# Graph attention on one core: scores and weights in one SBUF tile, one exponential in place, and a second PSUM bank for the transposes

## The chip, the core and the metric

The kernel runs on one core of a Trainium2 chip. The time is the device time of one execution in microseconds (us). A kernel is timed in several runs, and the median counts. One further execution is taken by the hardware profiler; the profile and the trace are of that one.

The core has five engines that run their own instruction streams and wait for each other by semaphores: PE (TensorE, matmul; PEld is its loading of the stationary operand), DVE (VectorE), ACT (ScalarE), POOL (GpSimd) and SP (SyncE, which here only issues transfers). Two on-chip memories matter here: SBUF, where most tiles live, and PSUM, where PE writes its products; the kernel divides PSUM by banks.

## The reference, cut to what matters

`x` has 16 batches of 1024 rows of 512, `adj` is one 1024 x 1024 matrix of zeros and ones that all batches share. There are 8 heads of 64.

```python
h = jnp.maximum(_layernorm(x, axis=-1), 0.0)
q = (h @ Wq + bq).reshape(b, n, H, HD)          # k and v alike
scores = jnp.einsum('bihd,bjhd->bhij', q, k) / jnp.sqrt(jnp.float32(HD))
scores = scores + mask[None, None, :, :]        # mask: -1e9 where adj == 0
weights = jax.nn.softmax(scores, axis=-1)
out = x + jnp.einsum('bhij,bjhd->bihd', weights, v).reshape(b, n, H * HD)
```

## The kernel before

A row of `adj` has few ones, so the kernel doesn't form the full matrix of scores. At the start it sorts the rows by their number of neighbours and makes a list of neighbours for each row. The sorted rows form 8 tiles of 128; tile 0 has the rows with most neighbours, up to 11 slots per row there and 2 in tile 7 (`CAPS`, line 41). What doesn't fit in tile 0's slots is cut into pieces of 4 neighbours, up to 128 pieces, which form a tile of their own (number -1 in `UNITS`, line 47).

**Per batch** the kernel does this. Each tile of `x` is loaded (`load_x`, line 558), normalised (`stats`, `variance`, `power`, `shift` and `norm`, lines 568 to 599; `norm` is on ACT), transposed by PE into a PSUM bank (`flip`, line 601: four transposes) and copied to SBUF by ACT (`unflip`, line 608). From the transposed tile PE makes keys and values (`proj_kv`, line 618), ACT copies them to SBUF (`evict_kv`), and SP stores them to a table in device memory (`store_kv`, line 629). There are three such tables, used in turn.

Then come 14 **units** (`UNITS`), each 2 to 4 neighbour slots of one tile. For a unit:

- `queries` (line 779): PE makes the tile's queries, in PSUM.
- `gather` (line 790): POOL gathers one row of keys and values per slot by an indirect transfer; the row's own slot comes by a plain transfer from SP. A unit's rows go into one of 6 buffers `g`.
- `multiply` (line 804) and `score` (line 809): DVE multiplies keys by the query and sums each head's 64 products. The sums go into the tile `scores`, **one PSUM bank for all slots of all units**.
- `exponent` (line 814): ACT takes the exponential. For tiles 7 to 4 (`SHARES`, in all batches but the last) it does so in place, in PSUM. For the others it writes the exponential to the SBUF tile `weights`, and then takes it **a second time**, in place in PSUM, for those slots that DVE will weigh.
- For tiles 7 to 4, `row_sums` (line 882) and `share` (line 825) on DVE turn exponentials into shares at once, from PSUM into `weights`.
- `weigh_s` (line 837): ACT multiplies a slot's values by its weight, 8 instructions of 64 columns. `weigh_v` (line 830): DVE does this for one slot of most units, reading the factors from `weights` (tiles 7 to 4) or from `scores` in PSUM (the others).
- `fold` (line 843) and `join` (line 848) add slots on DVE and POOL; tile 0, its pieces, and in the last batch all tiles, are added by PE in a PSUM bank instead (`add_up`, line 854, pool `acc` of two banks).
- `row_sums`, `scale` (line 892), `residual` on POOL and `put_out` finish a tile.

The pieces need a path of their own: `more` (line 874) on DVE sums the pieces' exponentials, and `pass_on` (line 879), a matmul of 8 columns on PE, brings these sums to the rows that own the pieces. It writes them into one extra column group of the `scores` bank, from where `row_sums` of tile 0 reads them.

**The order.** All engines' streams are written out in advance. `plan_of` (line 168) lists each operation with its engine, an assumed length, a **place** and what it needs; a unit of place is one of the 14 units, so a batch is 14. `Plan.ordered` (line 93) then plays it through: whenever an engine is free, it takes the ready operation of lowest place whose buffers are free (`POOLS`, line 72, says how many each pool has). The result is a fixed sequence per engine. At run time an instruction that must wait holds all that stand behind it on its engine. The plan knows of buffers but not that `scores` is one bank; semaphores are put in afterwards, by which data and which banks two instructions share.

The PSUM pools have eight banks: transposes 1 (`pht`), keys and values 2, queries 2, accumulators 2, `scores` 1.

## Time and profile before

| | |
|---|---|
| median of 3 runs | 1873.38 us (1863.66 to 1876.34) |
| the profiled execution | 1871.36 us |
| its span, first to last instruction | 1869.7 us |
| mean granted PE clock | 0.951 of full speed |
| instructions | 19763 |
| moved by DMA | 539.98 MB, 289 GB/s in the mean |

How to read the lines of the profile: a group of instructions has its line in the kernel, engine, operation, the tiles it writes `<-` reads, the shapes and `xcount`; then the busy time and the mean length of one in ns; then how long its engine sat idle just before these instructions, and what ended that (`<-ACT scores L823` means: an instruction of line 823 on ACT that writes `scores`). A timeline row has start, length, engine, line, operation, tiles, and in brackets the idle time before it. A row of a table by stretches has the stretch, its length, the busy time and number of instructions of PE, PEld, DVE, ACT and POOL, the granted clock, the share of the DMA engines, and GB/s. In a list of waits each row has who waited for whom, the total in us, how often, and the longest. A line that begins with `x624: 933/947/2034` gives least, median and greatest length in ns.

### The profile page before, as it was taken

The page shows a single profiled execution, that of the slowest core. Times are in us where ns is not written, and L with a number is a line of the kernel's source. Part 1 is how long each engine was busy: PE and PEld are TensorE (multiplying, and loading weights), DVE is VectorE, ACT ScalarE, POOL GpSimd, SP SyncE. Part 2 cuts the span into 40 slices and gives each one's busy share as a digit, 9 for nine tenths or more (in the row PEclk, how much of TensorE's full clock was granted, in tenths as well). Part 3 has the DMA queues.
Part 4 walks back from the last instruction along what each step waited for, and adds up shares of the span by engine and source line. Part 5 has one row for each costly group of instructions (what it writes and reads, how often), then busy time and mean ns, then how long its engine had stood idle before and what let it go on. Part 6 is the DMA issues. An engine that isn't in the chain of part 4 may idle for free. (4 is left out here: it accounts for less than half of the span.)

```text
span 1869.7 us, 19763 instructions
## 1 busy us (share of the span) xinstructions
PE 1653.7 (88%) x4301; PEld 762.9 (41%) x4301; DVE 1542.8 (83%) x1887; ACT 1508.6 (81%) x5661; POOL 1290.3 (69%) x1230
## 2 busy tenths in 40 slices
PE   5968699897989889897999979998898979989795
PEld 2434344443444444343444434444443434434331
DVE  5767779878898888988888788888888888889886
ACT  4337788889898888988887899988788888889864
POOL 4545668776787767776786867777676767767573
PEclk9989899998999999998999989999998999999898
DMA  5365789887898888888898878989787888988793
GB/s 214 119 254 200 289 301 315 317 295 281 307 333 313 314 301 298 299 293 295 304 336 308 294 275 306 327 313 326 271 314 270 300 304 310 329 285 315 264 329 134
DMA packets 151783, 539.98 MB, mean 289 GB/s; under 512 B 18908, under 2 KB 18908, under 8 KB 151656
## 3 DMA queue, kind: packets, MB, share of 16 engines
q0 software_dynamic: 111888, 399.09, 60.5%
q1 hardware_dynamic: 39768, 139.56, 20.6%
q8 instruction: 36, 0.59, 0.1%
q14 instruction: 91, 0.75, 0.1%
HBM read 437.85 MB, written 100.72 MB: 288 GB/s over the span
## 5 line engine op out<-in xcount | busy, mean ns | idle before, releaser
L841 ACT ACTIVATE g<-g,weights 128x64 f32<-128x64 f32 x4768 | 1185.4, 339 | 27.5 <-issue 15.8
L797 POOL DMA_INDIRECT g<-kv,index x624 | 628.7, 1007 | 248.7 <-issue 180.2
L616 PE MATMUL pq<-wq,hT 128*128 128x512 f32 x1024 | 471.0, 603 | 0.0
L807 DVE TENSOR_TENSOR g<-g,pq 128x2048 f32<-128x2048 f32 (+2 forms) x208 | 396.9, 1912 | 72.8 <-PE pq L616 42.9
L812 DVE TENSOR_REDUCE scores<-g 128x32 f32<-128x2048 f32 (+2 forms) x224 | 433.8, 1937 | 26.8 <-ACT scores L823 18.9
L616 PE MATMUL pk<-wk,hT 128*128 128x512 f32 x960 | 443.8, 606 | 0.0
L616 PE MATMUL pv<-wv,hT 128*128 128x512 f32 x960 | 431.6, 592 | 0.0
L846 DVE TENSOR_TENSOR g<-g 128x512 f32<-128x512 f32 (+1 forms) x285 | 267.0, 938 | 52.9 <-ACT g L841 39.1
L616 PEld LDWEIGHTS pq<-wq,hT 128*128 128x128 f32 x1024 | 200.2, 196 | 226.2 <-issue 221.2
L616 PEld LDWEIGHTS pk<-wk,hT 128*128 128x128 f32 x960 | 188.6, 196 | 211.7 <-issue 207.1
L616 PEld LDWEIGHTS pv<-wv,hT 128*128 128x128 f32 x960 | 182.4, 190 | 215.7 <-issue 212.4
L846 POOL TENSOR_TENSOR g<-g 128x512 f32<-128x512 f32 x105 | 137.4, 1308 | 111.2 <-DVE g L846 106.3
L908 POOL DMA_INDIRECT out_dram<-x,perm x128 | 137.6, 1075 | 79.1 <-DMA out_dram<-x,perm 28.4
L606 PE MATMUL pht<-ident,h 128*128 128x128 f32 x512 | 92.2, 310 | 86.5 <-ACT h L599 54.4
L564 POOL DMA_INDIRECT x<-in_x_dram,perm x128 | 136.6, 1067 | 36.1 <-issue 31.1
L606 PEld LDWEIGHTS pht<-ident,h 128*128 128x128 f32 x512 | 69.9, 159 | 168.0 <-ACT h L599 73.8
L864 PE MATMUL acc<-g,ident 128*128 128x512 f32 x176 | 101.3, 687 | 21.7 <-POOL g L846 12.1
L599 ACT ACTIVATE h<-x,shift,rstd 128x512 f32<-128x512 f32 x120 | 93.3, 809 | 32.4 <-DVE shift L589 31.3
L611 ACT COPY hT<-pht 128x512 f32<-128x512 f32 x128 | 74.1, 579 | 51.4 <-PE pht L606 27.4
L905 POOL TENSOR_TENSOR x<-x,o 128x512 f32<-128x512 f32 x68 | 90.0, 1324 | 21.9 <-DVE o L896 21.1
L627 ACT COPY kvt<-pk 128x512 f32<-128x512 f32 x120 | 68.9, 574 | 41.7 <-PE pk L616 33.6
L835 DVE TENSOR_TENSOR g<-g,scores 128x512 f32<-128x512 f32 (+1 forms) x104 | 73.8, 710 | 30.6 <-ACT scores L823 28.0
(226 smaller groups left out, 1196.6 us busy)
## 6 DMA issues: line engine op xcount, KB each, us to landing
g<-kv SPq DMA_DIRECT2D x128, 512.0 KB
kv<-kvt SPq DMA_DIRECT2D x120, 512.0 KB
g<-kv,index POOLq DMA_INDIRECT x624
adj<-in_adj_dram SPq DMA_DIRECT2D x8, 512.0 KB
x_first<-in_x_dram SPq DMA_DIRECT2D x8, 256.0 KB
x<-in_x_dram,perm POOLq DMA_INDIRECT x128
out_dram<-x,perm POOLq DMA_INDIRECT x128
wk<-in_L_gnn_Wk_dram SPq DMA_DIRECT2D x1, 1024.0 KB
```

What stands on the lines that cost most here:

```text
L564: nc.gpsimd.indirect_dma_start(out=X[n][:], out_offset=None, in_=x_rows, in_offset=on(ap=perm[:, t : t + 1], axis=0), element_offset=b * N * D
L599: nc.scalar.activation(HN[n], X[n], AF.Relu, bias=shift, scale=scale)
L606: nc.tensor.transpose(PH[n][:, c, :], hn[:, ts(c, P)], ident)
L616: nc.tensor.matmul(pt, HT[n][:, c, :], W[name][:, c, :], start=False, stop=(c == DC - 1))
L797: nc.gpsimd.indirect_dma_start(out=G[i][:, s].rearrange("p j d -> p (j d)"), out_offset=None, in_=KV[b % len(KV)][:], in_offset=on(ap=inde ...
L807: nc.vector.tensor_tensor(k, k, Q[b, t][:, None, :].to_broadcast([P, count, D]), ALU.mult)
L812: nc.vector.tensor_reduce(sc, heads(G[i][:, :count, 0, :]), AX.X, ALU.add)
L841: nc.scalar.activation(v[:, h, :], v[:, h, :], AF.Identity, scale=weights[:, c + s, h : h + 1])
L846: engine.tensor_tensor(v[:, 0:n], v[:, 0:n], v[:, first : first + n], ALU.add)
L864: nc.tensor.matmul(ACC[b, home], owner_t if t < 0 else ident, v[:, s, :], start=(u == parts_of(home)[0] and s == 0), stop=(u == parts_of(h ...
L905: nc.gpsimd.tensor_tensor(rows, rows, add, ALU.add)
L908: nc.gpsimd.indirect_dma_start(out=out_rows, out_offset=on(ap=perm[:, t : t + 1], axis=0), in_=X.pop(b * NT + NT - 1 - t)[:], in_offset=No ...
```

## The change

- `scores` goes: the pool of its PSUM bank too. `score` writes into the SBUF tile `weights`, `exponent` takes one exponential in place there for every unit, and `share`, `weigh_v` and `row_sums` read it there.
- `pass_on` writes into a tile of its own from the pool of the two accumulator banks.
- The freed bank goes to the transposes: `pht` has two.
- In the plan, lengths and places are changed: of the normalising (`stats`, `variance`, `power`, `norm`, `flip`), of keys and values, gathers, exponentials, sums, weighings, folds, joins, `add_up`, residuals and scaling. Some places of the preparation at the start move as well (`list_of`, `long_rows`, `longest`, `pieces`), which the diff leaves out.

```diff
@@ -69,7 +69,7 @@
 BY_VECTOR_LAST = {2: 1, 3: 1, 4: 2}
-POOLS = dict(x=14, h=2, pht=1, hT=11, pkv=2, kvt=3, q=2, q0=1, g=6, acc=2, o=1)
+POOLS = dict(x=14, h=2, pht=2, hT=11, pkv=2, kvt=3, q=2, q0=1, g=6, acc=2, o=1)
@@ -207,42 +207,42 @@
...
         b, j = divmod(n, NT)
-        p = (b - 1) * NU + j * rate if b > 0 else j * rate - 9.58 if b == 0 else 1.5 * j - 42.00
+        p = (b - 1) * NU + j * rate if b > 0 else j * rate - 16.21 if b == 0 else 1.5 * j - 41.10
         if n >= 0:
             known = [("perm_of",)] if b == 0 else []
-            add(("load_x", n), "POOL", 1.35, p - 7.27, known, [("x", n)], delay=4.5, moves=0.75)
+            add(("load_x", n), "POOL", 1.35, p - 8.07, known, [("x", n)], delay=4.5, moves=0.75)
         if b:
-            add(("stats", n), "DVE", 0.87, p - 3.48, [("load_x", n)], [("x", n)])
+            add(("stats", n), "DVE", 0.87, p - 4.39, [("load_x", n)], [("x", n)])
         if b and n % 2:
-            add(("variance", n // 2), "DVE", 0.22, p - 5.75, [("stats", n - 1), ("stats", n)])
-            add(("power", n // 2), "POOL", 0.86, p - 4.54, [("variance", n // 2)])
+            add(("variance", n // 2), "DVE", 0.22, p - 4.81, [("stats", n - 1), ("stats", n)])
+            add(("power", n // 2), "POOL", 0.86, p - 4.76, [("variance", n // 2)])
             add(("shift", n // 2), "DVE", 0.18, p - 4.40, [("power", n // 2)])
-        add(("norm", n), "ACT", 0.81, p - 4.09, [("shift", n // 2) if b else ("load_x", n)], [("x", n), ("h", n)])
-        add(("flip", n), "PE", 0.50, p - 3.76, [("norm", n)], [("h", n), ("pht", n)])
-        add(("unflip", n), "ACT", 0.58, p - 2.76, [("flip", n)], [("pht", n), ("hT", n)])
+        add(("norm", n), "ACT", 0.81, p - 4.41, [("shift", n // 2) if b else ("load_x", n)], [("x", n), ("h", n)])
+        add(("flip", n), "PE", 0.50, p - 4.02, [("norm", n)], [("h", n), ("pht", n)])
+        add(("unflip", n), "ACT", 0.58, p - 2.77, [("flip", n)], [("pht", n), ("hT", n)])
         if b == 0:
...
         for w in range(2):
-            e = p - 0.87 + 0.3 * w
+            e = p - 0.33 + 0.3 * w
             ready = [("unflip", n)]
...
             add(("proj_kv", n, w), "PE", 3.66, e, ready, [("hT", n), ("pkv", n, w)])
-            add(("evict_kv", n, w), "ACT", 0.58, e - 0.40, [("proj_kv", n, w)], [("pkv", n, w), ("kvt", n)])
+            add(("evict_kv", n, w), "ACT", 0.58, e - 0.52, [("proj_kv", n, w)], [("pkv", n, w), ("kvt", n)])
         ready = [("evict_kv", n, w) for w in range(2)]
@@ -270,29 +270,29 @@
             if is_own(u, s):
-                add(slot, "SP", 0.1, i - 2.54, stored if b == 0 else [("store_kv", n)], [g], delay=2.5, moves=1.5)
+                add(slot, "SP", 0.1, i - 1.94, stored if b == 0 else [("store_kv", n)], [g], delay=2.5, moves=1.5)
                 continue
-            add(slot, "POOL", 1.35, i - 4.03 + 0.1 * s, stored, [g], delay=4.0, moves=1.5)
+            add(slot, "POOL", 1.35, i - 4.33 + 0.1 * s, stored, [g], delay=4.0, moves=1.5)
         vector = by_vector(b, B, count)
...
         shares = shares_in(b, B, t)
-        add(("exponent", i), "ACT", 0.2 if shares or not vector else 0.36, i + 0.12, [("score", i)])
+        add(("exponent", i), "ACT", 0.22, i + 0.15, [("score", i)])
         weights = ("exponent", i)
...
             weights = ("share", i)
-            add(("row_sums", b, t), "DVE", 0.45, i + 0.64, [("exponent", i)])
-            add(weights, "DVE", 0.2, i + 0.01, [("row_sums", b, t)])
+            add(("row_sums", b, t), "DVE", 0.45, i + 0.31, [("exponent", i)])
+            add(weights, "DVE", 0.2, i + 0.52, [("row_sums", b, t)])
         weighed = []
...
             weighed.append(("weigh_v", i))
-            add(("weigh_v", i), "DVE", 0.15 + 0.533 * vector, i + 1.52, [weights], [g])
+            add(("weigh_v", i), "DVE", 0.30 + 0.533 * vector, i + 1.41, [weights], [g])
         for s in range(count - vector):
...
             on_pool = n[1] == 1 and u in POOL_FOLDS
-            add(("fold", i, *n), "POOL" if on_pool else "DVE", 1.4 if on_pool else 0.4 + 0.43 * n[1], i + 1.02, weighed, [g])
+            add(("fold", i, *n), "POOL" if on_pool else "DVE", 1.4 if on_pool else 0.4 + 0.43 * n[1], i + 0.79, weighed, [g])
             weighed = [("fold", i, *n)]
@@ -302,15 +302,15 @@
                 added = [("join", i)]
-                add(("join", i), "DVE", 0.69, i + 1.96, weighed + summed, [g, acc])
+                add(("join", i), "DVE", 0.69, i + 2.37, weighed + summed, [g, acc])
             summed = added
         else:
-            add(("add_up", i), "PE", 0.88 * (1 if folds(b, B, count) else count), i + 1.08, weighed, [g, acc])
+            add(("add_up", i), "PE", 0.88 * (1 if folds(b, B, count) else count), i + 0.33, weighed, [g, acc])
             added = [("add_up", b * NU + v) for v in parts]
...
             if shares:
-                add(("residual", b, home), "POOL", 1.35, i + 3.80, weighed, [g, ("x", n)])
+                add(("residual", b, home), "POOL", 1.35, i + 5.54, weighed, [g, ("x", n)])
                 add(("put_out", b, home), "POOL", 1.4, i + 2.40, [("residual", b, home)], [("x", n)], delay=4.0, moves=0.75)
@@ -319,10 +319,10 @@
                 add(("more", b), "DVE", 0.22, pieces[0] + 0.57, [("exponent", v) for v in pieces])
-                add(("pass_on", b), "PE", 0.3, pieces[0] + 1.41, [("more", b)])
+                add(("pass_on", b), "PE", 0.3, pieces[0] + 1.41, [("more", b)], [("acc", b, "more")])
                 exps.append(("pass_on", b))
-            add(sums, "DVE", 0.45 if home else 0.7, i + 0.13, exps)
-            add(("scale", b, home), "DVE", 0.69, i + 1.02, [sums] + added, [acc, o])
+            add(sums, "DVE", 0.45 if home else 0.65, i + 0.70, exps, [] if home else [("acc", b, "more")])
+            add(("scale", b, home), "DVE", 0.69, i + 0.42, [sums] + added, [acc, o])
             add(("residual", b, home), "POOL", 1.35, i + 2.75, [("scale", b, home)], [o, ("x", n)])
@@ -390,7 +390,6 @@
         ps_a = pool("ps_a", POOLS["acc"], space=psum)
-        ps_w = pool("ps_w", 1, space=psum)
@@ -747,8 +746,7 @@
                 nc.vector.tensor_reduce(number, free[:, first:end], AX.X, ALU.add)
-                for made in (scores, weights) if t in SHARES else (weights,):
-                    nc.vector.tensor_copy(made[:, end, :], number.to_broadcast([P, H]))
+                nc.vector.tensor_copy(weights[:, end, :], number.to_broadcast([P, H]))
             if not later:
@@ -761,8 +759,6 @@
-
-        scores = ps_w.tile([P, SLOTS + 1, H], F32, tag="w", name="scores")
         weights = const.tile([P, SLOTS, H], F32, tag="weights", name="weights")
@@ -808,30 +804,22 @@
             b, t, w, c, count = unit(i)
-            sc = scores[:, w, :]
-            nc.vector.tensor_reduce(sc, heads(G[i][:, :count, 0, :]), AX.X, ALU.add)
+            nc.vector.tensor_reduce(weights[:, w, :], heads(G[i][:, :count, 0, :]), AX.X, ALU.add)
...
             b, t, w, c, count = unit(i)
-            if shares_in(b, B, t):
-                nc.scalar.activation(scores[:, w, :], scores[:, w, :], AF.Exp, scale=HD**-0.5)
-                return
-            nc.scalar.activation(weights[:, w, :], scores[:, w, :], AF.Exp, scale=HD**-0.5)
-            n = by_vector(b, B, count)
-            if n:
-                own = scores[:, c + count - n : c + count, :]
-                nc.scalar.activation(own, own, AF.Exp, scale=HD**-0.5)
+            nc.scalar.activation(weights[:, w, :], weights[:, w, :], AF.Exp, scale=HD**-0.5)
...
             inv = INV.pop((b, t))[:, None, :].to_broadcast([P, count, H])
-            nc.vector.tensor_tensor(weights[:, w, :], scores[:, w, :], inv, ALU.mult)
+            nc.vector.tensor_tensor(weights[:, w, :], weights[:, w, :], inv, ALU.mult)
...
             v = heads(G[i][:, count - n : count, 1, :])
-            own = (weights if shares_in(b, B, t) else scores)[:, c + count - n : c + count, :, None]
+            own = weights[:, c + count - n : c + count, :, None]
             nc.vector.tensor_tensor(v, v, own.to_broadcast([P, n, H, HD]), ALU.mult)
@@ -869,7 +857,7 @@
-        MORE = {}
+        MORE, P_MORE = {}, {}
@@ -877,15 +865,15 @@
         def pass_on(b):
-            nc.tensor.matmul(scores[:, SLOTS, :], owner_t, MORE.pop(b), start=True, stop=True)
+            P_MORE[b] = ps_a.tile([P, H], F32, tag="acc", name=f"p_more_{b}")
+            nc.tensor.matmul(P_MORE[b], owner_t, MORE.pop(b), start=True, stop=True)
...
             c = first_col[t, 0]
-            made = scores if shares_in(b, B, t) else weights
-            nc.vector.tensor_reduce(s, made[:, c : c + CAPS[t] + 1, :].rearrange("p s h -> p h s"), AX.X, ALU.add)
+            nc.vector.tensor_reduce(s, weights[:, c : c + CAPS[t] + 1, :].rearrange("p s h -> p h s"), AX.X, ALU.add)
             if t == 0:
-                nc.vector.tensor_tensor(s, s, scores[:, SLOTS, :], ALU.add)
+                nc.vector.tensor_tensor(s, s, P_MORE.pop(b), ALU.add)
             INV[b, t] = small.tile([P, H], F32, tag="inv", name=f"inv_{b}_{t}")
```

8 lines of the change are left out of this document (4 added, 4 removed).

## The prediction

> **What bounds the kernel now.** I read the busy times first, then the steady stretch from 300 to 1620 us (the first and the last batch differ), then who waited for whom.
>
> ```profile
> PE 1653.7 (88%) x4301; PEld 762.9 (41%) x4301; DVE 1542.8 (83%) x1887; ACT 1508.6 (81%) x5661; POOL 1290.3 (69%) x1230
> ```
>
> ```profile
> 300.00:1620.00 1320.00, 1211.40 (x3157) 559.81 (x3157) 1123.68 (x1325) 1139.74 (x4326) 963.83 (x901) 0.96 0.86 305
> ```
>
> In the steady stretch PE is busy 1211.4 of 1320 us (92%), ACT 86%, DVE 85%, POOL 73%, the DMA engines 86%. No engine is full: the kernel is a ring of engines that wait for each other. PE has the least room, so I ask first what leaves PE idle (total, times, longest):
>
> ```profile
> PE pht L606 <- ACT h L599: 54.4, 19, 5.3
> PE scores L880 <- DVE g L835: 37.4, 6, 6.5
> PE scores L880 <- DVE scores L812: 13.3, 4, 4.7
> PE pht L606 <- ACT hT L611: 15.4, 16, 2.3
> PE pht_first L606 <- ACT hT_first L611: 3.9, 2, 3.0
> PE scores L880 <- DVE more L877: 1.9, 2, 1.7
> ```
>
> The change touches two of these at their root: the small matmul that passes the pieces' sums on (L880), and the transposes (L606) that wait until the only transpose bank is emptied (L611). The largest, transposes that wait for a normalised tile, changes only in its place.
>
> **pass_on.** What does L880 really wait for? DVE and PE around one of the six long waits, and around one of the other four:
>
> ```profile
> 862.57 2.29 DVE L812 TENSOR_REDUCE scores<-g 128x32 f32<-128x2048 f32 x1 [0.81 <-ACT scores L823]
> ...
> 871.04 2.29 DVE L812 TENSOR_REDUCE scores<-g 128x32 f32<-128x2048 f32 x1 [1.06 <-ACT scores L823]
> ...
> 878.99 2.29 DVE L812 TENSOR_REDUCE scores<-g 128x32 f32<-128x2048 f32 x1 [1.15 <-ACT scores L823]
> ...
> 884.67 0.21 DVE L877 TENSOR_REDUCE more<-weights 128x8 f32<-128x40 f32 x1
> ```
>
> ```profile
> 885.62 0.57 PE L880 MATMUL scores<-more,owner_t 128*128 128x8 f32 x2 [6.48 <-DVE g L835]
> ```
>
> ```profile
> 1424.71 0.22 DVE L877 TENSOR_REDUCE more<-weights 128x8 f32<-128x40 f32 x1 [1.44 <-ACT weights L819]
> ```
>
> ```profile
> 1427.25 0.39 PE L880 MATMUL scores<-more,owner_t 128*128 128x8 f32 x2 [2.41 <-DVE scores L812]
> ```
>
> Its data are ready when `more` ends, at 884.88, but it writes into the bank of `scores` and so also waits for the DVE instruction behind `more` that uses that bank. That part is 885.62 - 884.88 = 0.74 us in the first case and 1427.25 - 1424.93 = 2.32 us in the second. With a tile of its own it goes: 6 x 0.74 + 4 x 2.32 = 13.7 us. The rest of the 6.48 us is waiting for `more` itself, and stays unless DVE comes to it earlier. DVE lost 0.81 + 1.06 + 1.15 = 3.02 us shortly before it, in reductions that wait for the exponential of **another** unit; the data don't ask for that, the shared bank does. I let PE have these as well: 6 x 3.02 = 18.1 us. Together -31.8 us. Bounds: -13.7 if DVE's earlier arrival meets another wait, and -52.6 (37.4 + 13.3 + 1.9) if `more` is always early enough.
>
> The new tile adds a wait of its own: it takes one of the two accumulator banks, so pass_on waits for the `scale` that freed it, with add_up and the next queries behind it on PE. In all batches but the last only tile 0 accumulates in PSUM, so that bank came free a batch ago: nothing. In the last batch it is tile 1's, scaled at place 9.42 against 12.41 for pass_on: three units, nothing either; with no such lead it would cost one wait of a few us, once.
>
> **Transposes.** With two banks PE fills the second while ACT empties the first: 15.4 + 3.9 = -19.3 us. The other bound is 0: the next transpose then waits for its normalised tile instead.
>
> **One exponential, and operands in SBUF.**
>
> ```profile
> L835 DVE TENSOR_TENSOR g<-g,scores 128x512 f32<-128x512 f32 x97 | 65.3, 674 | 30.3 <-ACT scores L823 28.0 <-ACT weights L819 0.9 <-PE scores L880 0.8
> L835 DVE TENSOR_TENSOR g<-g,weights 128x512 f32<-128x512 f32 x45 | 36.8, 817 | 0.3
> L896 DVE TENSOR_TENSOR o<-g,inv 128x512 f32<-128x512 f32 x45 | 30.7, 681 | 0.1
> L611 ACT COPY hT<-pht 128x512 f32<-128x512 f32 x128 | 74.1, 579 | 51.4 <-PE pht L606 27.4 <-remote 11.4 <-PE pq L616 8.1
> L475 ACT CAST bq_parts<-scratch 128x512 bf16<-128x512 f32 x1 | 0.6, 614 | 0.0
> L886 DVE TENSOR_REDUCE sums<-scores 128x8 f32<-128x40 f32 x30 | 5.8, 194 | 10.2 <-ACT scores L817 10.2
> L886 DVE TENSOR_REDUCE sums<-weights 128x8 f32<-128x40 f32 x2 | 0.4, 214 | 0.0
> ```
>
> ```profile
> L823 ACT ACTIVATE scores<-scores 128x8 f32<-128x8 f32 (+1 forms) x104 | 16.9, 162 | 18.7 <-remote 12.2 <-ACT weights L819 3.4
> L846 DVE TENSOR_TENSOR g<-g 128x512 f32<-128x512 f32 (+1 forms) x285 | 267.0, 938 | 52.9 <-ACT g L841 39.1 <-issue 6.7 <-remote 5.1
> L797 POOL DMA_INDIRECT g<-kv,index x624 | 628.7, 1007 | 248.7 <-issue 180.2 <-ACT scores L817 12.7 <-POOL x L905 10.9
> ```
>
> ```profile
> L797 POOL DMA_INDIRECT g<-kv,index x624: 933/947/2034, 99.3 to 1833.0; - x156
> ```
>
> ACT loses the 104 second exponentials, -16.9 us. The 224 that stay read SBUF instead of PSUM; the nearest pair is a copy of 512 from PSUM (579 ns) and a cast of 512 from SBUF (614 ns), so +35 ns each, +7.8 us. ACT gets 9.1 us lighter; I count nothing for it, since ACT waits for PE and DVE anyway. If that cover is gone, it is a gain.
>
> DVE: 104 weighings (L835) take their factors from SBUF. The row for that exists: 817 ns against 674 with factors in PSUM, so 104 x 0.143 = +14.9 us. The other bound is L896, also with two SBUF operands, at 681 ns: 104 x 0.007 = +0.7. I take 817, the same line and operands. The 60 row sums of the sharing tiles go from 194 to 214 ns, 60 x 0.020 = +1.2 us. The 60 shares (L828) have no row of their own kind: 0 by L896, at most 60 x 0.143 = 8.6 by L835; I take 0, as they are as short as a few slots. For the score reductions into SBUF I take 0, and at most the same 20 ns: 224 x 0.020 = 4.5 us.
>
> [...]
>
> POOL: its gathers last 1007 ns in the mean and 947 in the median, 624 x 0.060 = 37.4 us that they are held up. If DVE's operations with two SBUF operands do that (267.0 + 36.8 + 30.7 = 334.5 us of them), each microsecond costs 0.11. The change adds 104 x 0.674 + 60 x 0.181 (L828's mean, row in rival 5) = 81.0 us of them: +9.1 us. Bounds 0 and, were POOL hit as hard as the 817 ns row, 14.9. I count 9.1 whole, as the gathers of a batch's first units have no cover (below).
>
> **The moved places.** A unit of place is a fourteenth of a batch; `more` came at 884.67 and, five batches on, at 1424.71, so a unit is 540.04 / 5 / 14 = 7.7 us. Statistics move 0.91 units (7.0 us) earlier and the normalising 0.32 (2.5 us), which can only help the 54.4 us above; the K and V projections move 0.54 units (4.2 us) later, past the next batch's first query projection. I count 0 for both and make each a rival. The residual of the sharing tiles moves 1.74 units later and holds its gather buffer longer; POOL takes what is ready, so I take 0 for that too.
>
> **The sum:** -31.8 - 19.3 + 14.9 + 1.2 + 9.1 = -25.9 us. The profiled execution took 1871.4 us (span 1869.7), so 1845.5; the median of the runs lies 2.0 us above it: 1847.5 us.
>
> **Rivals.** (1) *The port.* DVE's weighings hold up POOL and are held up by it, so DVE comes to `more` no earlier: pass_on gives only 13.7, and shares and reductions cost their upper bounds: -13.7 - 19.3 + 14.9 + 1.2 + 8.6 + 4.5 + 9.1 = +5.3, 1878.7 us. For it speak 817 against 674; against it the 681. [...]
>
> (2) *The transposes' gain is hidden anyway*, since the next normalised tile is late too: -25.9 + 19.3 = -6.6, 1866.8 us. For it speaks that 54.4 us wait for such tiles.
>
> (3) *The next batch's gathers come late; slower.* A batch's first gathers need all eight stores of its keys and values:
>
> ```profile
> 881.37 0.32 SPq L639 DMA_DIRECT2D kv<-kvt  x1
> ```
>
> ```profile
> 887.44 0.96 POOL L797 DMA_INDIRECT g<-kv,index  x1 [0.30 <-issue]
> ```
>
> ```profile
> 894.29 1.22 DVE L807 TENSOR_TENSOR g<-g,pq 128x1024 f32<-128x1024 f32 x1 [0.21 <-DMA g<-kv,index]
> ```
>
> ```profile
> 992.65 0.97 POOL L797 DMA_INDIRECT g<-kv,index  x1 [0.35 <-issue]
> ```
>
> ```profile
> 1002.56 1.22 DVE L807 TENSOR_TENSOR g<-g,pq 128x1024 f32<-128x1024 f32 x1 [3.74 <-PE pq L616]
> ```
>
> ```profile
> 875.33 0.38 PE L614 MATMUL pv<-bv_parts,chosen 128*128 128x512 bf16 x1
> 875.55 3.60 PE L616 MATMUL pv<-wv,hT 128*128 128x512 f32 x8
> ```
>
> One projection (875.33 to 879.15) is 3.8 us. Where the multiply already waits for the gather (894.29) it all shows; where it waits for the query (1002.56), the gather, landing 894.29 - 887.44 = 6.85 us after its issue, would end at 992.65 + 3.8 + 6.85 = 1003.3, 0.7 us later. With the two kinds in turn, 7 x 3.8 + 8 x 0.7 = 32.2 us over 15 boundaries, and DVE, late there, comes late to `more` too, so the 18.1 us are void: -25.9 + 32.2 + 18.1 = +24.4, 1897.8 us. It decides once the last store comes over 2 us later against the batch before it. Against it: the last projections still stand ahead of pass_on, whose stall shrinks.
>
> (4) *More than counted.* The earlier statistics also take half of the 54.4 us: 1847.5 - 27.2 = 1820.3 us. The clock works the same way: right behind the long stall PE's granted clock was 0.77 for 9.4 us, 2.2 us lost:
>
> ```profile
> 885.60:895.00 9.40, 9.38 (x26) 5.15 (x27) 7.38 (x9) 6.84 (x25) 6.73 (x8) 0.77 0.82 277
> ```
>
> (5) *It doesn't do what it says:* the one tile is tracked as a whole, and each reduction waits for the weighings queued ahead, eight activations of a slot (8 x 1185.4 / 4768 = 2.0 us): 224 x 2.0 = +446, beyond 2300 us. Against it: the shares write the old `weights` tile between its readers and never waited for these:
>
> ```profile
> L841 ACT ACTIVATE g<-g,weights 128x64 f32<-128x64 f32 x4768 | 1185.4, 339 | 27.5 <-issue 15.8 <-DVE weights L828 9.6 <-DVE g L846 0.6
> L828 DVE TENSOR_TENSOR weights<-scores,inv 128x32 f32<-128x32 f32 (+2 forms) x60 | 10.9, 181 | 4.6 <-ACT scores L817 3.4
> ```
>
> **How the numbers follow.** Forecast 0.42, (1) 0.15, (2) 0.12, (3) 0.19, (4) 0.10, (5) 0.02. The forecast's own range is 1830 to 1865. The whole range is 1812 to 1900: below it lies little beyond (4), above it (5) and the upper part of (3), and it holds the forecast with pass_on and transposes at their lesser bounds (1847.5 + 18.1 + 19.3 = 1884.9). A measurement tells about 1% (18.7 us) from no change. Faster by more than that: most of the forecast (0.35) and (4), 0.45. Within it: the rest of the forecast, (1) and (2), 0.34. Slower: (3) and (5), 0.21.
>
> **What would show it.** Right: L812 waits no longer for exponentials (its 26.8 us below fall to a few); PE's wait at pass_on falls from 52.6 to about 21 and names only `more`; transposes no longer wait for L611; ACT has 104 instructions fewer; L835 has a mean near 817 ns. Wrong: pass_on's wait stays near 40 us or more (DVE is no earlier); DVE's multiply at the start of most batches waits 2 us or more for a gather instead of 0.21 (rival 3); L835 above 0.85 us or gathers above 1.05 us in the mean (rival 1).
>
> ```profile
> L812 DVE TENSOR_REDUCE scores<-g 128x32 f32<-128x2048 f32 (+2 forms) x224 | 433.8, 1937 | 26.8 <-ACT scores L823 18.9 <-ACT weights L819 3.1 <-ACT scores L817 2.6
> ```

## The result, and the profile after

The changed kernel takes 1806.53 us (median of 4 runs, 1801.24 to 1808.46) against 1873.57 us (4 runs) of the kernel before on the same chip: ratio 0.9639, 95% interval 0.9599 to 0.968. That is 67 us less. The forecast was 1847.5 us, 25.9 us less, with a range from 1812: the sign was right, the size 2.6 times too small.

The changed kernel's page and its row of the steady stretch (PE, PEld, DVE, ACT, POOL, clock, DMA share, GB/s):

```profile
PE 1643.0 (91%) x4301; PEld 756.7 (42%) x4301; DVE 1560.5 (86%) x1883; ACT 1495.7 (83%) x5557; POOL 1322.7 (73%) x1230
```

```profile
300.00:1620.00 1320.00, 1246.57 (x3274) 573.47 (x3273) 1185.25 (x1377) 1176.07 (x4430) 1031.55 (x937) 0.97 0.88 317
```

PE executes the same 4301 matmuls in a span of 1806.0 us instead of 1869.7. Of the 63.7 us, 10.7 are PE's busy time (1653.7 to 1643.0, the granted clock is 0.959 for 0.951), and 53.0 are idle time of PE (1869.7 - 1653.7 = 216.0, and 1806.0 - 1643.0 = 163.0). In the steady stretch PE gets through 3274 matmuls instead of 3157, and every engine does more per microsecond.

Where along the span? `more` runs once a batch, so its first and last start (in the source view, before and after) date the batches:

```profile
L877 DVE TENSOR_REDUCE more<-weights x16: 208/210/223, 232.2 to 1837.5; 128x8 f32<-128x40 f32 x16
```

```profile
L865 DVE TENSOR_REDUCE more<-weights x16: 205/210/218, 225.5 to 1774.4; 128x8 f32<-128x40 f32 x16
```

The 15 batches between take 1605.3 us before and 1548.9 after: 56.4 us, 3.8 us a batch. The start gives 6.7, the tail 0.6.

PE's waits in the changed kernel (total, times, longest):

```profile
PE acc L852 <- POOL g L834: 64.1, 16, 8.1
PE pht L605 <- issue: 20.4, 3, 19.2
PE pht L605 <- ACT h L598: 18.7, 12, 5.7
...
PE pk L615 <- ACT hT L610: 9.2, 13, 0.8
...
PE acc L852 <- ACT g L829: 4.1, 3, 2.5
...
PE p_more L869 <- DVE more L865: 0.6, 1, 0.6
```

Read it by sums, not by names. The pass-on's wait is gone (52.6 to 0.6), but `add_up` now stands in front of it on PE and waits 64.1 us for a fold on POOL, 12.1 before. Both together with `add_up`'s wait for ACT: 52.6 + 12.1 + 5.5 = 70.2 before, 0.6 + 64.1 + 4.1 = 68.8 after. In this trace that stall has changed its name and given nothing. The idle time that went is the transposes': 54.4 for normalised tiles became 18.7, and 15.4 + 3.9 for their bank became 0, of which 9.2 come back one step later, where the K projection waits for the tile just evicted.

The names hang on the execution, though. A later trace of the same kernel, on the third chip of the experiments, has these two rows:

```profile
PE pht L605 <- ACT h L598: 55.9, 22, 21.2
PE acc L852 <- POOL g L834: 47.7, 18, 7.3
```

The 21.2 us are one wait ahead of the first `more`, which in the list above stands as 19.2 us under "issue" (no cause in the profile). What repeats is a sum: the waits of transposes into `pht` but those for their bank, of `add_up` and of pass_on, whatever ended them, are 111 us here and 112 there, against 145 and 150 in the two traces of the kernel before. I call it the **common sum** below.

The groups that the change touches, all in the changed kernel:

```profile
L793 POOL DMA_INDIRECT g<-kv,index x624 | 631.7, 1012 | 208.2 <-issue 154.1 <-POOL x L893 15.1 <-PE acc L852 9.0
...
L807 DVE TENSOR_REDUCE weights<-g 128x32 f32<-128x2048 f32 (+2 forms) x224 | 430.9, 1924 | 0.7
...
L811 ACT ACTIVATE weights<-weights 128x32 f32<-128x32 f32 (+2 forms) x224 | 49.4, 220 | 47.4 <-DVE weights L807 42.7 <-issue 4.5
...
L884 DVE TENSOR_TENSOR o<-g,inv 128x512 f32<-128x512 f32 x45 | 40.1, 892 | 17.6 <-POOL x L893 17.6
...
L816 DVE TENSOR_TENSOR weights<-weights,inv 128x32 f32<-128x32 f32 (+2 forms) x60 | 19.9, 332 | 0.5
```

and two of them by form:

```profile
L834 DVE TENSOR_TENSOR g<-g 128x1024 f32<-128x1024 f32 x105 | 162.0, 1543 | 6.9 <-ACT g L829 6.4 <-DVE weights L807 0.6
...
L823 DVE TENSOR_TENSOR g<-g,weights 128x512 f32<-128x512 f32 x142 | 99.4, 700 | 1.3 <-issue 0.9
```

Before, the same fold and the join beside it had these rows, the join going to 829 ns after:

```profile
L846 DVE TENSOR_TENSOR g<-g 128x1024 f32<-128x1024 f32 x105 | 134.2, 1278 | 21.7 <-ACT g L841 17.0 <-issue 4.2
...
L852 DVE TENSOR_TENSOR g<-g,g 128x512 f32<-128x512 f32 x45 | 30.7, 682 | 0.1
```

The reductions lost their waits (26.8 to 0.7 us), ACT has one exponential for each of the 224 units and 104 instructions fewer (5557 for 5661), and weighings cost 700 ns in the mean, not the 817 I took. Instead the long folds, joins, scale (681 to 892 ns in the mean) and shares (181 to 332) are longer, and DVE's busy time is up by 17.7 us in all.

### The profile page after: what moved, and what is told of

Its sections match the earlier page's. It is cut to its first block, busy times and chain, and to the rows that moved or that the text cites. A ratio compares the mean times of both kernels' runs of the same rounds, so it can differ in the third digit from the quotient of the medians.

```text
span 1806.0 us, 19695 instructions
## 1 busy us (share of the span) xinstructions
PE 1643.0 (91%) x4301; PEld 756.7 (42%) x4301; DVE 1560.5 (86%) x1883; ACT 1495.7 (83%) x5557; POOL 1322.7 (73%) x1230
## 5 line engine op out<-in xcount | busy, mean ns | idle before, releaser
L793 POOL DMA_INDIRECT g<-kv,index x624 | 631.7, 1012 | 208.2 <-issue 154.1
L615 PE MATMUL pq<-wq,hT 128*128 128x512 f32 x1024 | 463.8, 596 | 0.0
L615 PE MATMUL pk<-wk,hT 128*128 128x512 f32 x960 | 443.5, 605 | 11.5 <-ACT hT L610 9.2
L807 DVE TENSOR_REDUCE weights<-g 128x32 f32<-128x2048 f32 (+2 forms) x224 | 430.9, 1924 | 0.7
L834 DVE TENSOR_TENSOR g<-g 128x512 f32<-128x512 f32 (+1 forms) x285 | 286.5, 1009 | 20.9 <-ACT g L829 17.4
L615 PEld LDWEIGHTS pq<-wq,hT 128*128 128x128 f32 x1024 | 196.0, 191 | 225.9 <-issue 222.0
L896 POOL DMA_INDIRECT out_dram<-x,perm x128 | 149.3, 1167 | 97.8 <-DMA out_dram<-x,perm 46.1
L563 POOL DMA_INDIRECT x<-in_x_dram,perm x128 | 145.9, 1140 | 39.5 <-issue 31.0
L852 PE MATMUL acc<-g,ident 128*128 128x512 f32 x176 | 102.4, 699 | 70.2 <-POOL g L834 63.7
L834 POOL TENSOR_TENSOR g<-g 128x512 f32<-128x512 f32 x105 | 139.8, 1331 | 31.9 <-DVE g L834 15.4
L605 PE MATMUL pht<-ident,h 128*128 128x128 f32 x512 | 88.5, 314 | 40.2 <-issue 20.4
L626 ACT COPY kvt<-pk 128x512 f32<-128x512 f32 x120 | 69.0, 575 | 59.4 <-issue 21.2
L823 DVE TENSOR_TENSOR g<-g,weights 128x512 f32<-128x512 f32 (+1 forms) x149 | 108.5, 728 | 1.3 <-issue 0.9
```

Source lines behind the costliest of these rows:

```text
L563: nc.gpsimd.indirect_dma_start(out=X[n][:], out_offset=None, in_=x_rows, in_offset=on(ap=perm[:, t : t + 1], axis=0), element_offset=b * N * D
L605: nc.tensor.transpose(PH[n][:, c, :], hn[:, ts(c, P)], ident)
L615: nc.tensor.matmul(pt, HT[n][:, c, :], W[name][:, c, :], start=False, stop=(c == DC - 1))
L793: nc.gpsimd.indirect_dma_start(out=G[i][:, s].rearrange("p j d -> p (j d)"), out_offset=None, in_=KV[b % len(KV)][:], in_offset=on(ap=inde ...
L807: nc.vector.tensor_reduce(weights[:, w, :], heads(G[i][:, :count, 0, :]), AX.X, ALU.add)
L823: nc.vector.tensor_tensor(v, v, own.to_broadcast([P, n, H, HD]), ALU.mult)
```

## The experiments

The same kernel before took 1824 to 1897 us on the chips that ran the experiments. So kernels are compared on one chip at a time; each of the five groups below ran on a chip of its own. My theory at this point was that the bank waits make the gain (theory A); the rival (theory B) was that the moved places make it.

### First chip: the parts one after another

The kernel before took 1886.14 us here (13 runs).

**Scores in SBUF, pieces' sums alone in the old bank**; places, both exponentials and one transpose bank as before.

```diff
-        scores = ps_w.tile([P, SLOTS + 1, H], F32, tag="w", name="scores")
+        scores = const.tile([P, SLOTS, H], F32, tag="scores", name="scores")
+        p_more = ps_w.tile([P, H], F32, tag="w", name="p_more")
...
-            nc.tensor.matmul(scores[:, SLOTS, :], owner_t, MORE.pop(b), start=True, stop=True)
+            nc.tensor.matmul(p_more, owner_t, MORE.pop(b), start=True, stop=True)
...
```

> The kernel before with its whole plan, and one thing changed: scores is a tile in SBUF, and the pieces' sums go to a PSUM bank of their own. Both exponentials stay, one transpose bank, no instruction changes its order. Theory A (the gain comes from waits that the shared bank made): score reductions no longer wait for exponentials, pass_on no longer for the bank, about 20 to 40 us faster, 1835 to 1855. Theory B (the gain comes from the moved places): within 10 us of before, as each stall only turns up one instruction later.

1849.90 us, ratio 0.9793 (0.9734 to 0.9853): -36.2 us, within theory A's 1835 to 1855. Its waits and its weighings with factors from the new tile:

```profile
PE p_more L881 <- DVE more L878: 31.2, 8, 5.1
...
PE pht L606 <- ACT hT L611: 19.0, 15, 2.4
```

```profile
L836 DVE TENSOR_TENSOR g<-g,scores 128x512 f32<-128x512 f32 x97 | 81.5, 840 | 10.8 <-ACT scores L824 10.7
```

The whole edit gave about what the pass_on term alone had said (31.8), in part by luck: pass_on's own waits fell by 21.4 us (52.6 in the first trace of the kernel before, 31.2 here), and the rest came elsewhere. The reductions' waits fell to 0.7 us here too, and the weighings of one slot, 840 ns in the mean instead of 674, did not stop the gain.

**One tile, one exponential** as well; all functions of the change, places of before, one transpose bank, the pieces' sums in a bank of their own (the diff is against the changed kernel, its places left out).

```diff
-POOLS = dict(x=14, h=2, pht=2, hT=11, pkv=2, kvt=3, q=2, q0=1, g=6, acc=2, o=1)
+POOLS = dict(x=14, h=2, pht=1, hT=11, pkv=2, kvt=3, q=2, q0=1, g=6, acc=2, o=1)
...
-            P_MORE[b] = ps_a.tile([P, H], F32, tag="acc", name=f"p_more_{b}")
+            P_MORE[b] = ps_w.tile([P, H], F32, tag="w", name=f"p_more_{b}")
...
```

> As the run before it, and also one tile for scores and weights and one exponential in place: ACT has 104 instructions fewer (16.9 us less busy, some 8 given back for reading SBUF). Order as before otherwise. Theory A: another 5 to 10 us faster than that run, if ACT's length counts. Theory B: the same as that run within 5 us.

1838.86 us, ratio 0.9721 (0.9655 to 0.9787). The runs (1831.96 to 1852.47) overlap with those of the kernel above, so the 11 us between the medians aren't settled; no loss from dropping the second exponential shows.

**The whole change but its places.**

```diff
-            add(("stats", n), "DVE", 0.87, p - 4.39, [("load_x", n)], [("x", n)])
+            add(("stats", n), "DVE", 0.87, p - 3.48, [("load_x", n)], [("x", n)])
...
```

> All of the change but for lengths and places in the plan: two transpose banks, the pieces' sums in an accumulator bank, and the plan's old numbers; the order shifts only as far as the second bank lets transposes start sooner. Theory A: most of the 67 us is here, 1815 to 1835, transposes no longer wait for their eviction (19.3 us before). Theory B: less than a third of it, 1850 or more.

1858.19 us, ratio 0.9841 (0.9782 to 0.99): 19.3 us slower than the kernel above, which has one transpose bank but also another bank for the pieces' sums. No transpose waits for an eviction, but transposes wait 127.4 us for normalised tiles. Theory A has no place for that.

**The places alone**, on the kernel before.

```diff
-            add(("stats", n), "DVE", 0.87, p - 3.48, [("load_x", n)], [("x", n)])
+            add(("stats", n), "DVE", 0.87, p - 4.39, [("load_x", n)], [("x", n)])
...
```

> The kernel before (scores in a PSUM bank, two exponentials, one transpose bank) with the lengths and places of the plan after. Theory A: within 15 us of before, perhaps slower, as the bank's waits stay. Theory B: most of the gain without any of the new tiles, 1825 to 1840; transposes wait for normalised tiles some 20 us instead of 54.

1868.22 us, ratio 0.9906 (0.9873 to 0.994): -17.9 us, between the two theories, and transposes still wait 44.1 us for normalised tiles. No part alone gives 0.9639. The places and the one-tile kernel multiplied would (0.9721 x 0.9906 = 0.963); the places and the kernel with two banks, which are the actual parts of the change, would not (0.9841 x 0.9906 = 0.9749). So the parts interact.

### Second chip: places and second bank apart

The kernel before took 1823.72 us here (7 runs).

**New places, one transpose bank** (the one-tile kernel above with the plan of the change):

```diff
-            add(("stats", n), "DVE", 0.87, p - 3.48, [("load_x", n)], [("x", n)])
+            add(("stats", n), "DVE", 0.87, p - 4.39, [("load_x", n)], [("x", n)])
...
```

> One tile, one exponential, the pieces' sums in a bank of their own, and the places of the changed kernel, but one transpose bank (the kernel that ran at 0.9721 of the time before, with other places). Theory 'the second bank pays only together with the new places': without it the transposes still wait for L611 of the kernel before, some 20 us, and the ratio stays near 0.972 to 0.976, about 1% above the changed kernel's 0.9639. Rival 'the places pay by themselves, the second bank nothing': 0.962 to 0.967, as the changed kernel. Rival 'the gains add up' (0.9721 times the 0.9906 of the places alone): 0.963, with the second bank worth nothing either.

**Old places, one transpose bank, pieces' sums with the accumulators:**

```diff
-POOLS = dict(x=14, h=2, pht=2, hT=11, pkv=2, kvt=3, q=2, q0=1, g=6, acc=2, o=1)
+POOLS = dict(x=14, h=2, pht=1, hT=11, pkv=2, kvt=3, q=2, q0=1, g=6, acc=2, o=1)
```

> The kernel that ran at 0.9721 (one tile, one exponential, old places, one transpose bank), with one difference: the pieces' sums go to one of the two accumulator banks, as in the changed kernel. It splits the loss from 0.9721 to 0.9841 between the accumulator bank and the second transpose bank. Theory 'the second transpose bank made the loss': 0.970 to 0.975, and transposes wait some 45 us for normalised tiles, as without it. Rival 'the accumulator bank made it': 0.980 or more, with PE waiting at the pass-on matmul or at add_up for an accumulator to come free.

**Places of the normalising chain alone, and all others alone**, each on the whole change with old places:

```diff
-            add(("stats", n), "DVE", 0.87, p - 3.48, [("load_x", n)], [("x", n)])
+            add(("stats", n), "DVE", 0.87, p - 4.39, [("load_x", n)], [("x", n)])
...
```

```diff
-            add(("scale", b, home), "DVE", 0.69, i + 1.02, [sums] + added, [acc, o])
+            add(("scale", b, home), "DVE", 0.69, i + 0.42, [sums] + added, [acc, o])
...
```

> All of the changed kernel but its places, of which it has only those of the chain load of x, statistics, variance, power, shift, normalising, transposes, eviction (the kernel with none of them ran at 0.9841 and its transposes waited 127.4 us for normalised tiles). Theory 'the normalised tiles come too late for two banks': that wait falls to 20 to 50 us and the ratio to 0.962 to 0.972. Rival 'the other places make the difference' (K and V projections, add_up, scale, row sums, residual): 0.980 to 0.986, and the wait stays above 100 us or moves to the accumulators.

> The counterpart: all of the changed kernel, with the places of the chain from the load of x to the transposes' eviction as before, and all other places new. Theory 'the normalised tiles come too late for two banks': transposes wait over 100 us for them and the ratio is 0.978 to 0.986. Rival 'the other places make the difference': 0.962 to 0.970.

Measured, in this order: 1810.11 us, 0.9914 (0.9887 to 0.9942); 1795.61, 0.9853 (0.9831 to 0.9875); 1795.67, 0.9852 (0.983 to 0.9874); 1802.61, 0.9884 (0.9863 to 0.9906). All expectations were set against ratios of the first chip, and on this one the kernel before was 62 us faster. So none of them is decided. The changed kernel itself and the one with old places and two banks did not run here. What can be read is that with one bank the new places were no gain on this chip: the first kernel is 14.5 us slower than the second (1803.69 to 1812.64 against 1794.38 to 1799.19), though the two also differ in the pieces' bank. The next chip repeats what matters side by side.

### Third chip: the whole change beside two of its variants

The kernel before took 1897.36 us here (13 runs), and 1886.87 us in a second series (10 runs), ratio 0.9949 (0.9919 to 0.9978): the same text, so some 10 us between two kernels are not to be told apart on this chip.

> The changed kernel itself, beside its own variants, because the kernel before took 1886.1 us on the chip of the first four experiments and 1823.7 us on that of the next four, so ratios of different calls can't be set against each other. Theory 'the size of the gain hangs on the chip' (where the kernel before runs slow, its stalls are longer and more is won): on a chip where the kernel before takes about 1824 us the ratio is 0.983 to 0.990, and where it takes 1870 to 1890 us it is 0.960 to 0.970. Rival 'the gain is the same everywhere': 0.960 to 0.968 on any chip.

> All of the changed kernel with the places of before and one transpose bank, on the same chip as the next one. Theory 'with old places the second transpose bank costs time': this one is 1% or more faster than the one with two banks. Rival 'the loss seen with two banks was the chip': both within 0.4%. Theory 'new places and second bank do nothing together': this one within 0.4% of the changed kernel; theory 'they make a third of the gain': the changed kernel is 1% faster.

> All of the changed kernel with the places of before and two transpose banks. Theory 'old places and two banks don't go together': transposes wait over 100 us for normalised tiles, as before (127.4 us), and the kernel is 1% or more above the one with one bank. Rival 'it was the chip': that wait is below 50 us and the two are within 0.4%.

> The kernel before itself, for a trace of this chip. Theory 'chips differ in how PE's waits fall': on a chip where it takes about 1824 us, PE's waits at the pass-on matmul and for normalised tiles (52.6 and 54.4 us in the first trace) are 30 to 50 us less in sum. Rival 'chips differ in the clock alone': the waits are as in the first trace within 10 us, and PE's busy time is shorter.

- The change: 1813.58 us, 0.956 (0.9499 to 0.9621).
- Old places, one transpose bank: 1850.64 us, 0.9729 (0.9674 to 0.9783).
- Old places, two banks: 1856.52 us, 0.9764 (0.9713 to 0.9816).

The whole change and the last differ in the plan's places and lengths alone: **42.9 us**, runs 1807.14 to 1823.61 against 1850.00 to 1862.32. In their two traces the common sum falls from 152 to 112 us, and PE's idle time from 213.4 to 169.5 (each trace lacks some 50 of the 4301 matmul records). The two with old places differ by the second bank alone: 5.9 us (0.3%) the wrong way, with overlapping runs, so a second bank gives nothing with these places, and a loss through it isn't shown either. Places and second bank together are worth 37.1 us.

The change took 0.9682, 0.9639 and 0.956 of the time before in the three series that have it (fourth chip, the result, this one), lowest where the kernel before is slowest, as in my first theory; but neighbouring intervals overlap, and on a chip near 1824 us it never ran, so this is not shown. The trace of the kernel before has the waits of the first one (37.4 + 14.0 at pass_on, 51.9 for normalised tiles); there is no trace of it on the second chip.

With old places and two banks, this wait heads PE's list, and the next rows are one instance of it on the timeline, with the rows between left out:

```profile
PE pht L605 <- ACT h L598: 123.2, 36, 8.5
```

```profile
873.84 0.16 DVE L581 TENSOR_SCALAR rstd<-mv 128x2 f32<-128x2 f32 x1
...
881.29 0.73 POOL L584 TENSOR_TENSOR rstd<-rstd,minus_half 128x2 f32<-128x2 f32 x1
...
884.27 1.24 DVE L588 SCALAR_TENSOR_TENSOR shift<-mv,rstd 128x2 f32<-128x2 f32 x1
...
885.55 1.52 ACT L598 ACTIVATE h<-x,shift,rstd 128x512 f32<-128x512 f32 x2 [2.46 <-DVE shift L588]
...
886.41 1.12 PE L605 MATMUL pht<-ident,h 128*128 128x128 f32 x4 [8.54 <-ACT h L598]
```

Read from the bottom. PE waits 8.54 us for a normalised tile, ACT for DVE's shift, the shift stands behind DVE's work, and POOL takes the power 7.3 us after the variance is there, behind a gather, a residual, a fold, a store and a load. The same steps at the same batch's end in the changed kernel:

```profile
851.71 0.15 DVE L581 TENSOR_SCALAR rstd<-mv 128x2 f32<-128x2 f32 x1
...
853.93 0.72 POOL L584 TENSOR_TENSOR rstd<-rstd,minus_half 128x2 f32<-128x2 f32 x1
...
855.71 0.15 DVE L588 SCALAR_TENSOR_TENSOR shift<-mv,rstd 128x2 f32<-128x2 f32 x1
...
855.86 1.72 POOL L834 TENSOR_TENSOR g<-g 128x512 f32<-128x512 f32 x1 [1.21 <-DVE shift L588]
...
857.59 1.51 ACT L598 ACTIVATE h<-x,shift,rstd 128x512 f32<-128x512 f32 x2
...
857.64 1.13 PE L852 MATMUL acc<-g,ident 128*128 128x512 f32 x2 [2.48 <-POOL g L834]
...
858.60 0.28 PE L869 MATMUL p_more<-more,owner_t 128*128 128x8 f32 x2
...
858.74 1.59 PE L605 MATMUL pht<-ident,h 128*128 128x128 f32 x8
```

POOL takes the power 2.1 us after the variance, and the transposes follow without a wait of their own. PE's wait is 2.48 us, at `add_up`. The two instances are far apart: 8.54 us is the longest of these waits, and the 16 at `add_up` in the changed kernel average 4.0 us (64.1 / 16). Over the 14 inner batches, the power that follows the last variance before `more` comes 5.4 us after it in the median with old places and two banks, and 2.1 us in the changed kernel. The shift comes 4.7 us behind the start of `more` in the one, and 0.7 us ahead of it in the other.

### Fourth chip: which places, and what the rest of the stall is

The kernel before took 1865.16 us here (7 runs). The two halves of the places were run again beside the change, and one kernel more:

```diff
-POOL_FOLDS = (2, 3, 8, 9, 10, 11, 12)
+POOL_FOLDS = (2, 3, 8, 9, 11, 12)
```

> The changed kernel as the anchor for the next three, since the kernel before ran at 1824 to 1897 us on the chips so far and ratios of different calls can't be set against each other. Both theories: 0.956 to 0.964 on a chip where the kernel before takes 1870 us or more; on one of about 1824 us, 0.980 to 0.992.

> All of the changed kernel but its places, with the new places of the chain from the load of x to the transposes' eviction alone. Theory 'the earlier normalised tiles make the part of the gain that the old places lack': within 0.5% of the changed kernel, batches of about 104 us. Rival 'the other places make it': 1.5% or more above the changed kernel, as with all places old (0.9764 against 0.956), batches of about 108 us.

> The counterpart: the chain's places as before, all other places new. Theory 'the earlier normalised tiles make it': 1.5% or more above the changed kernel, with transposes waiting 100 us or more for normalised tiles. Rival 'the other places make it': within 0.5% of the changed kernel.

> The changed kernel with the fold of tile 0's first unit on DVE instead of POOL (the fold for which PE waited 64.1 us at add_up, 16 times). Theory 'the stall is that of the batch's end, whatever PE meets first': the wait of about 3 to 5 us a batch shows under another name (transposes for normalised tiles, or pass_on for more) and the time is within 0.7% of the changed kernel's. Rival 'it is that fold': PE's waits at add_up fall below 20 us, no other grows, and the kernel is 1% or more faster than the changed one. DVE takes 16 folds of about 0.9 us more.

- The change: 1806.78 us, 0.9682 (0.9636 to 0.9728).
- Places of the chain alone: 1816.08 us, 0.9736 (0.9689 to 0.9782).
- All other places alone: 1823.39 us, 0.9751 (0.9692 to 0.9809).
- The fold of tile 0's first unit on DVE: 1818.28 us, 0.9743 (0.9686 to 0.98).

The chain's places come to within 9.3 us of the change, a little more than the 0.5% that I had set. The other places do better than the theory allowed: 0.9% above the change and not 1.5%, and transposes wait 22.6 us for normalised tiles, not 100. By the common sum it is 113 us in the change, 135 with the chain's places and 123 with the others. So either half comes within 1% of the whole, where on the third chip the lack of both cost 2.4%; a kernel with all places old did not run here. PE's list in the second half:

```profile
PE acc L852 <- POOL g L834: 83.7, 15, 8.7
PE pht L605 <- ACT h L598: 22.6, 12, 7.1
```

Moving the fold that PE waited for:

```profile
PE pht L605 <- ACT h L598: 56.8, 18, 5.7
PE acc L852 <- issue: 43.0, 8, 7.8
...
PE acc L852 <- ACT g L829: 12.4, 5, 4.5
...
PE acc L852 <- POOL g L834: 1.4, 1, 1.4
```

The wait for POOL falls from 63.6 us in the change on this chip to 1.4, the others rise by more (the common sum goes from 113 to 132), and the kernel is 11.5 us slower: the stall belongs to the batch's end, not to that fold.

### Fifth chip: head or tail of the chain

The kernel before took 1872.60 us here (7 runs). Neither the change nor the kernel with all places old ran beside them. Both kernels are the whole change with old places; the first has new places for three operations (load, statistics, power), the second for the rest of the chain.

```diff
...
-            add(("stats", n), "DVE", 0.87, p - 3.48, [("load_x", n)], [("x", n)])
+            add(("stats", n), "DVE", 0.87, p - 4.39, [("load_x", n)], [("x", n)])
...
-            add(("power", n // 2), "POOL", 0.86, p - 4.54, [("variance", n // 2)])
+            add(("power", n // 2), "POOL", 0.86, p - 4.76, [("variance", n // 2)])
```

```diff
...
-        add(("norm", n), "ACT", 0.81, p - 4.09, [("shift", n // 2) if b else ("load_x", n)], [("x", n), ("h", n)])
+        add(("norm", n), "ACT", 0.81, p - 4.41, [("shift", n // 2) if b else ("load_x", n)], [("x", n), ("h", n)])
...
```

> All of the changed kernel with the places of before, but the load of x, the statistics and POOL's power at their new places (0.80, 0.91 and 0.22 units earlier); variance, normalising and transposes stay. In the kernel with all places old, the long wait at a batch's end ran back from the transposes over the normalising (ACT) and the shift (DVE) to POOL's power, which started 7.4 us after the variance was known. Theory 'that chain is late at POOL, and starting it earlier is enough': transposes' wait for normalised tiles falls from 123 to 127 us to below 50, batches of 104 to 106 us, and the kernel is 1% or more faster than the next one. Rival 'the normalising and the transposes have to move too': wait above 100 us, batches of 108 us.

> The rest of that chain: places of before, but the variance, the normalising, the transposes, their eviction and the first batch's offset at their new places; load of x, statistics and power as before. Theory 'the chain is late at POOL': the normalising, placed earlier, waits for the shift all the same, so transposes or ACT wait 100 us or more and batches take 108 us or more. Rival 'the normalising has to move': wait below 50 us and 104 to 106 us a batch, faster than the one with the statistics earlier.

1818.45 us, 0.9733 (0.9679 to 0.9788), against 1837.31 us, 0.985 (0.9786 to 0.9914). PE's two largest waits of the batch's end, and `more`, in the first and then in the second:

```profile
PE acc L852 <- POOL g L834: 90.4, 15, 9.1
PE pht L605 <- ACT h L598: 42.0, 18, 21.7
```

```profile
L865 DVE TENSOR_REDUCE more<-weights x16: 207/218/226, 223.2 to 1781.0; 128x8 f32<-128x40 f32 x16
```

```profile
PE pht L605 <- ACT h L598: 105.9, 33, 7.9
PE acc L852 <- POOL g L834: 21.4, 4, 7.9
```

```profile
L865 DVE TENSOR_REDUCE more<-weights x16: 207/210/223, 228.9 to 1797.8; 128x8 f32<-128x40 f32 x16
```

The head alone is 18.9 us faster than the tail alone, with runs apart (1815.24 to 1821.99 against 1833.39 to 1849.81). Of the 18.2 us between the spans, 11.1 lie in the 15 batches (103.9 against 104.6 us each), 5.7 in the start, 1.4 in the tail. The tail alone was expected at 108 us a batch or more, so that part of the theory failed.

The names again say too much: with the head, transposes wait 42.0 us for normalised tiles (21.7 of these are one wait) instead of 105.9, but `add_up` waits 90.4 instead of 21.4, at the same place, some 6 to 7 us after `more`. The common sum is 140 against 156 us. Nor does the trace show POOL earlier behind the variance: the power at the batch's end comes 6.3 us after it in the median with the head moved, more than the 5.4 us above, and the shift still 4.7 us behind `more`. So that the head is worth more than the tail is shown on this chip; that POOL's power is the step that makes the stall is not.

## Why the prediction was wrong in size

**The step that failed** is "which can only help the 54.4 us above [...] I count 0 for both". With two transpose banks and all else equal, the moved places are worth 42.9 us on one chip, and 17.9 us on the kernel before without the rest. They are the part of the change that the title leaves out. Rival 4 came nearest, the earlier statistics taking part of the waits for normalised tiles (54.4 to 18.7 in one trace), priced at 27.2 us with a chance of 0.10. The profile of before held a clue: the largest wait in PE's list was for normalised tiles, in a kernel whose PE has the least room, and I had written down that the statistics come 7.0 us earlier. I should have followed that wait back. Which step is late differs, though: in the kernel before, at the batch's end, POOL's power comes 3.6 us after the variance in the median, and DVE's shift another 5.2 us after the power. Which of the moved places matter, and through which step, stays open.

**A second step failed with it:** DVE's and POOL's longer instructions were charged to the end, +25.2 us in all. The kernel with scores in SBUF has these terms and the pass_on term alone, -6.6 us by my own figures, and measured -36.2.

Taking 42.9 us for the places, 0 for the second bank (below) and 0 for the weighings and gathers, my sum would be -31.8 - 42.9 = -74.7 us, an estimate across chips, against -67 measured. With places and second bank taken together (-37.1) it would be -68.9.

**pass_on, -31.8.** The edit by itself gave -36.2. Its waits fell to 31.2 us, where I expected 21, and the reductions' to 0.7. In the whole change the wait at pass_on is 0.6, but it moved to `add_up`, one instruction ahead, with about the same 69 us in the first trace. What remains is the lag of the other engines at a batch's end, and PE meets it with whatever it has first: pass_on (before), transposes (old places with two banks), `add_up` (after), transposes and `add_up` (fold on DVE).

**Transposes, -19.3.** The transposes' waits for their eviction are gone, as predicted, and with old places that gave nothing: rival 2's mechanism, the next tile is late too. With the new places the second bank's share isn't known: the kernel with one bank and new places never ran beside the change.

**Weighings, +14.9, row sums, +1.2, gathers, +9.1.** The 142 weighings of one slot take 99.4 us, and took 65.3 + 36.8 = 102.1: no dearer in sum. The row sums of 40 columns take 222 ns, where I took 214. The shares, for which I took 0 and at most 8.6 us, cost 9.0 more (10.9 to 19.9). Gathers rose from 1007 to 1012 ns, 3.0 us in all. DVE's busy time did rise by about what I had counted, 17.7 us, but in folds, joins, scale and shares, and it lies beside other work: the kernel whose weighings took 840 ns was 36 us faster than before. Rival 1 fell for the same reason; the port that it names was the author's assumption, and no run shows one.

DVE's scale was longer where it began beside a fold on POOL: in the changed kernel 10 of the 45 scales from SBUF took 1.61 to 1.62 us, each begun while such a fold ran, and the other 35 took 0.67 to 0.72. One of the ten is the scale beside POOL's fold of 855.86 to 857.58; from PSUM the mean is 683 ns:

```profile
856.52 1.62 DVE L884 TENSOR_TENSOR o<-g,inv 128x512 f32<-128x512 f32 x1
```

```profile
L884 DVE TENSOR_TENSOR o<-acc,inv 128x512 f32<-128x512 f32 x23 | 15.7, 683 | 9.3 <-PE acc L852 7.2 <-POOL x L893 1.2 <-issue 0.9
```

**Rival 3**, late gathers after a batch's start, did not come: DVE's multiplies wait 11.0 us for gathers in all, 1.3 at the longest. **Rival 5** did not either: no reduction waits for the weighings ahead.

**Open** is why the same text differs by chip. The kernel with old places, one bank and the sums in the accumulators has these `more` rows on the second and on the third chip:

```profile
L865 DVE TENSOR_REDUCE more<-weights x16: 208/214/226, 217.1 to 1759.4; 128x8 f32<-128x40 f32 x16
```

```profile
L865 DVE TENSOR_REDUCE more<-weights x16: 208/224/225, 232.7 to 1816.4; 128x8 f32<-128x40 f32 x16
```

That is 102.8 and 105.6 us a batch, at a granted clock of 0.965 and 0.947, while DVE's reductions (1920 ns in the mean) and ACT's weighings (338) take the same on both. PE's waits differ: for normalised tiles 20.5 and 41.6 us, in the common sum 96 and 136. That a lower clock tips the batch's end over is only argued. Open too is what lets the other places alone recover as much as they do. That `add_up` comes ahead of pass_on on PE doesn't suffice: it does so in the kernel with the tail alone as well, which took 1837 us.

## What to carry to other kernels

Where an order is written out in advance, price a moved operation by the wait at the end of its chain: follow PE's largest wait back step by step, and ask which step the move starts earlier. Then test that step by moving it alone; one instance on the timeline is not enough, as POOL's power shows. A freed buffer gave nothing here while what fills it came late; whether it pays with the earlier producer, no run shows. A stall at the end of a stage was here a lag of engines, not a property of the instruction that showed it (one fold moved, and the wait for it fell from 63.6 to 1.4 us while the common sum rose from 113 to 132): sum the waits of all instructions at that place before counting one as gained.

## What the runs showed of the hardware

The same kernel took 1824 to 1897 us on five chips, 4% apart, and two series of it on one chip came 0.5% apart. The ratio of the changed kernel to it went from 0.956 to 0.9682 over three series.

PE's granted clock was low behind a short stall too: 0.64 over the 9.4 us behind the wait of 2.48 us at `add_up`, in the changed kernel. The stretches before, in and behind it:

```profile
846.00:855.15 9.15, 9.15 (x23) 3.79 (x21) 9.12 (x9) 8.66 (x35) 7.85 (x7) 1.00 0.95 366
855.15:857.60 2.45, 0.01 (x1) 0.00 (x0) 2.45 (x5) 2.41 (x10) 1.72 (x1) 1.00 0.44 174
857.60:867.00 9.40, 8.59 (x21) 4.26 (x22) 9.37 (x10) 9.40 (x36) 7.11 (x7) 0.64 0.98 333
867.00:876.00 9.00, 9.00 (x23) 4.00 (x22) 5.71 (x10) 9.00 (x39) 5.76 (x7) 1.00 0.91 325
```

At 0.64 for 9.4 us, an estimated 3.4 us are lost (9.4 x 0.36), more than the wait itself and more than the 2.2 us behind the 6.48 us before. It doesn't follow each time: in the same trace PE was idle for 2.40 us up to 440.64, and the clock was 1.00 over the next 9.4 us.

A longer mean of one instruction did not go with a longer kernel: DVE's weighing of one slot had 700 ns here and 859 in the second chip's kernel with old places and one bank, which took 1795.61 us, less than the changed kernel's 1806.53.
